# A recurrent recommender on one core: zeros multiplied ahead of the first input, the item part of the attention in another PSUM ring, and the first inputs issued by ScalarE

## The chip, the cores and the metric

The kernel runs on one core of one Trainium2 chip. The metric is the device time of one execution in microseconds (us). The time before is the median of three runs, and one further execution was recorded by the hardware profiler.

## What is computed

For 1024 users with 100 steps of history each, 128 features wide, the reference runs a GRU over the history, scores every state against the candidate item with a small three-layer network, takes a softmax over the steps, pools the states with it, runs a second recurrent layer (AUGRU) whose update gate is weighted by the pooled vector, and puts the result through a three-layer head. Cut to what bears on the first microseconds:

```python
def gru_step(h, x_t):
    gi = x_t @ gru_Wih.T + gru_bih
    gh = h @ gru_Whh.T + gru_bhh
    i_r, i_z, i_n = jnp.split(gi, 3, axis=-1)
    h_r, h_z, h_n = jnp.split(gh, 3, axis=-1)
    r = jax.nn.sigmoid(i_r + h_r)
    z = jax.nn.sigmoid(i_z + h_z)
    n = jnp.tanh(i_n + r * h_n)
    h_new = (1.0 - z) * n + z * h
    return (h_new, h_new)
...
feat = jnp.concatenate([keys, q, keys - q, q * keys], axis=-1)
score = _mlp(feat, [(att_W0, att_b0), (att_W1, att_b1), (att_W2, att_b2)], jax.nn.relu)
score = jnp.where(mask[:, :, None] == 1, score, -jnp.inf)
attn = jax.nn.softmax(score, axis=1)[..., 0]
pooled = jnp.einsum('bt,btd->bd', attn, keys)
```

The part of the first attention layer that depends on the item q alone, `q @ (W_q - W_diff).T + b0`, is the same for all steps. The kernel computes it once; it is called the item part.

## The kernel before

Features lie on the 128 partitions and users on the free axis. The 1024 users are two halves of 512 (`HB`), and each step of the GRU phase works first on half 0, then on half 1. Everything is float32.

**The GRU phase** (`gru_phase`, line 186 on) loops over 100 steps. A step and half has three gates. `gate` (line 504 on) takes one buffer of the PSUM pool `ps` (six buffers, tag "g", called the gates' ring) and adds up one or two products in it: the input x with `wih` and the state h with `whh`. Each product is four matmuls, one for each 32 rows of the output (line 508). At step 0 there is no h, so a gate is one product. ScalarE makes the gates' sigmoid and tanh (lines 520, 539, 540), VectorE the rest of the step (lines 537 or 528, 538, 543 to 545). After the two halves of step s come the attention's matmuls for step s-1 (`attend`, line 670), in two buffers of a second PSUM pool `pa` (two buffers, tag "a"). VectorE adds the item part `q0` to their result one step later (`take`, line 704).

**The start.** SyncE issues the loads in the program's order: `wih` (line 188), x of step 0 for half 0 (line 191), the biases `bih` and `bhh` (line 124, called from 192 and 193), x of step 0 for half 1 (line 195), `whh`, then x of steps 1 and 2 (line 477), the item (line 226) and the attention's weights (lines 124 and 234 to 240). VectorE's first instruction adds the biases into `brz` (line 200). ScalarE's first are its table load and a one-column activation (line 204). GpSimd clears tiles (lines 201 to 215).

**The item part** (`item_part`, line 242 on) runs once, after the gates of step 1 and before the first attention matmuls. For each half it takes a buffer of `pa` for the product `pq` (line 245), and ScalarE copies it with a bias into `q0` (line 248).

**What sets the order.** There is no scheduler at work here (`tc.manual_schedule()`): on each engine the instructions stand in the order in which the Python code names them[...]. The tile framework only adds semaphore waits: for data, and for the buffer of a pool to come free. The pool `wp` (two buffers for each tag) holds VectorE's products `kq` (line 583), which the attention's matmuls read.

After step 99 come the last softmax blocks, the pooling, and the AUGRU phase with PSUM banks chosen by hand (`EARLY_BANKS`, `LATE_BANKS`, `FREE_BANK`). The diff touches none of that code.

Of the kernel before, what the change touches and what calls it, by code (L numbers as in the profile page):

```python
# [9 lines left out]
F32 = mybir.dt.float32  # L10
# [9 lines left out]
P = 128  # L20
B = 1024
T = 100
HB = 512
# [4 lines left out]
R = 32  # L28
# [50 lines left out]
def kernel(ctx: ExitStack, tc: tile.TileContext, a: dict, out: bass.AP):  # L79
# [26 lines left out]
    nc = tc.nc  # L106
# [79 lines left out]
    def gru_phase(pools):  # L186
# [1 line left out]
        nc.sync.dma_start(out=wih, in_=a["wih"])  # L188
        xp = pools.enter_context(tc.tile_pool(name="xp", bufs=8))
        x_first = xp.tile([P, HB], F32, name="x")  # L190
        nc.sync.dma_start(out=x_first, in_=a["hist_x"][0][:, :HB])
        bih = load("bih", [P, 3])
        bhh = load("bhh", [P, 3])
        x_second = xp.tile([P, HB], F32, name="x")
        nc.sync.dma_start(out=x_second, in_=a["hist_x"][0][:, HB:])
        whh = load("whh", [P, 3, P])
        pre = pools.enter_context(tc.tile_pool(name="pre", bufs=1))

# [20 lines left out]
        wp = pools.enter_context(tc.tile_pool(name="wp", bufs=2))  # L219
        sp = pools.enter_context(tc.tile_pool(name="sp", bufs=2))  # L220
        kp = pools.enter_context(tc.tile_pool(name="kp", bufs=3 * NH))
        ps = pools.enter_context(tc.tile_pool(name="ps", bufs=6, space=PSUM))
        pa = pools.enter_context(tc.tile_pool(name="pa", bufs=2, space=PSUM))

        def attention_weights():
            nc.sync.dma_start(out=item, in_=a["item"])
            w0 = load("w0", [P, 4, A0])
            for i in range(NH):
                for f, s in F0[i]:
                    nc.vector.tensor_add(wk[i][:, f], w0[:, 0, s], w0[:, 2, s])  # L230
                    nc.vector.tensor_copy(wkq[i][:, f], w0[:, 3, s])
                    nc.vector.tensor_sub(wq[i][:, f], w0[:, 1, s], w0[:, 2, s])
                    for f1, s1 in F1[i]:
                        nc.sync.dma_start(out=w12[i][f, f1], in_=a["w1"][s, s1])
                    nc.sync.dma_start(out=bm[i][f, :], in_=a["b0"][s, :])
                sc = slice(SC[i], SC[i] + 1)
                for f1, s1 in F1[i]:
                    nc.sync.dma_start(out=w12[i][f1, sc], in_=a["w2"][s1, :])
                    nc.sync.dma_start(out=bm[i][f1, :], in_=a["b1"][s1, :])
                nc.sync.dma_start(out=bm[i][sc, :], in_=a["b2"].partition_broadcast(1))  # L240

        def item_part():
            for i in range(NH):
                pq = pa.tile([P, HB], F32, tag="a", name="pq")
                nc.tensor.matmul(
                    pq, lhsT=wq[i], rhs=item[:, ts(i, HB)], start=True, stop=True
                )
                nc.scalar.activation(q0[:, ts(i, HB)], pq, AF.Identity, bias=bm[i])
# [211 lines left out]
        class Half:  # L460
# [13 lines left out]
            def load(self, t, again=False):  # L474
                if t or again:
                    x = xp.tile([P, HB], F32, name="x")
                    nc.sync.dma_start(out=x, in_=a["hist_x"][t][:, self.cols])
                    self.x[t] = x
# [100 lines left out]
            def product(self, t):  # L579

                h = self.h[t]
                kq = wp.tile([P, HB], F32, name="kq")
                nc.vector.tensor_mul(kq, h, item[:, self.cols])  # L583
                self.first = h, kq

# [238 lines left out]
        for s in range(T):  # L824
# [36 lines left out]
            if s == 0:  # L861
                attention_weights()
            else:
                if not staged:
                    next(rest, None)
                if s == 1:
                    item_part()
                attend(s - 1)
# [403 lines left out]
    with ExitStack() as pools, tc.manual_schedule():  # L1272
        gru_phase(pools)
# [79 lines left out]
```

## Time and profile before

| | us |
|---|---|
| median of three runs | 2031.93 |
| the three runs | 2027.62, 2031.93, 2031.96 |
| the profiled execution, whole | 2054.49 |
| its span, first to last instruction | 2052.7 |
| PE busy from 0 to 10 us | 6.03 |
| PE busy from 10 to 20 us | 10.00 |
| PE busy from 20 to 30 us | 8.36 |
| PE busy from 30 to 40 us | 10.00 |

PE is TensorE's matmuls, PEld its weight loads, DVE is VectorE, ACT ScalarE, POOL GpSimd, SPq and ACTq are the queues of SyncE and ScalarE in which DMAs are issued. Times in the profile count from the first instruction of the span. A timeline row gives the start, the length from the first start to the last end in the row, the engine, the source line, the operation with the tile it writes and those it reads, the shape, the count, and in brackets how long the engine had been idle and what ended that. A matmul in float32 shows as two records for one instruction, so that eight records are one product of a gate with one operand.

### The profile page before, as it was taken

To read this page: it belongs to the slowest core of one execution; us is meant where nothing else is said; L and a number is where in the kernel's file an instruction comes from. 1 tells how busy PE (TensorE), PEld (TensorE's weight loads), DVE (VectorE), ACT (ScalarE), POOL (GpSimd) and SP (SyncE) were. 2 spreads that over 40 slices of the span, in tenths; PEclk is the share of its full clock that TensorE was granted. 3 is DMA by queue.
4 is the path that set the end of the run, shared out by engine and by line. 5 is a ranking of instruction groups with operands and counts; after the bars stand their busy time and mean duration, and the time that the engine had idled before them with its cause. 6 is when DMAs were issued, how large, how long until landed. Compare 5 with 4: busy or idle time off the path is not lost.

```text
span 2052.7 us, 41040 instructions
## 1 busy us (share of the span) xinstructions
PE 1998.8 (97%) x15452; PEld 1049.1 (51%) x15452; DVE 1763.7 (86%) x3066; ACT 824.5 (40%) x1508; POOL 1313.0 (64%) x1291
## 2 busy tenths in 40 slices
PE   8999999999999999999999999998699999999998
PEld 4655433333455544444443333334344556679997
DVE  6888999998999999989999899997377777888886
ACT  3334343333434343434343343343244444445554
POOL 0234939569797969695979787998543354443431
PEclk9999999999999999999999999999799999999999
DMA  4453233332334334333433232333432333333332
GB/s 121 97 115 105 89 105 113 96 93 78 104 113 114 108 109 124 113 99 110 135 105 100 85 99 77 102 105 103 117 101 88 94 110 98 94 102 85 93 72 37
DMA packets 241643, 205.65 MB, mean 100 GB/s; under 512 B 59270, under 2 KB 204394, under 8 KB 241434
## 3 DMA queue, kind: packets, MB, share of 16 engines
q1 hardware_dynamic: 227498, 170.43, 29.4%
q0 software_dynamic: 12352, 32.31, 5.7%
q8 instruction: 123, 2.02, 0.4%
q14 instruction: 86, 0.70, 0.1%
q10 hardware_dynamic: 1584, 0.20, 0.1%
HBM read 146.82 MB, written 54.40 MB: 98 GB/s over the span
## 4 chain that ended last, share of the span: by engine, by line
PE 83%; DVE 9%; issue 2%; DMA 2%; ACT 1%; POOL 1%; another core or an unknown queue 1%; SPq 0%; DVEq 0%; ACTq 0%; POOLq 0%
PE ps L508 42%; PE pm L670 14%; PE ph L1076 5%; PE pr L1076 4%; PE pu L1076 4%; PE pr L1072 4%; PE pu L1072 4%; PE ph L1072 4%; DVE kq L583 1%; DMA rows<-keys_d,idx_k 1%; DVE ps L538 1%; DVE d L544 1%; DVE d L543 1%; DVE u L528 1%; ACT ps L539 1%
## 5 line engine op out<-in xcount | busy, mean ns | idle before, releaser
L508 PE MATMUL ps<-x,wih 128*32 128x512 f32 x4800 | 778.3, 595 | 4.6 <-DMA x<-in_hist_x 4.0
L508 PE MATMUL ps<-hn,whh 128*32 128x512 f32 x4752 | 768.1, 592 | 0.0
L508 PEld LDWEIGHTS ps<-x,wih 128*32 128x32 f32 x4800 | 260.2, 110 | 291.0 <-issue 270.2
L508 PEld LDWEIGHTS ps<-hn,whh 128*32 128x32 f32 x4752 | 258.2, 110 | 280.1 <-issue 271.9
L539 ACT ACTIVATE ps<-ps,bih 128x512 f32<-128x512 f32 x200 | 132.4, 662 | 546.5 <-DVE ps L538 546.5
L493 POOL TENSOR_TENSOR xm<-x,m 128x512 f32<-128x512 f32 x200 | 248.1, 1240 | 121.7 <-DMA m<-mask_d 60.8
L494 POOL TENSOR_TENSOR hist<-hist,xm 128x512 f32<-128x512 f32 x200 | 269.7, 1349 | 15.7
L174 POOL DMA_INDIRECT rows<-keys_d,idx_k x220 | 213.9, 972 | 86.5 <-POOL rows L173 50.0
L607 POOL TENSOR_TENSOR pooled<-pooled,kw 128x512 f32<-128x512 f32 x191 | 257.6, 1349 | 15.0
L670 PE MATMUL pm<-hn,wk 128*32 128x512 f32 x1200 | 257.1, 592 | 4.0 <-DVE f L704 2.3
L606 POOL TENSOR_TENSOR kw<-kt,e 128x512 f32<-128x512 f32 x191 | 220.1, 1153 | 62.2 <-DVE e L779 62.1
L670 PE MATMUL pm<-kq,wkq 128*32 128x512 f32 x1200 | 257.2, 592 | 0.0
L520 ACT ACTIVATE r<-ps,brz 128x512 f32<-128x512 f32 x200 | 137.6, 688 | 285.6 <-PE ps L508 285.1
L670 PE MATMUL pm<-mv,w 128*32 128x512 f32 (+1 forms) x808 | 240.5, 592 | 8.2 <-DVE e L760 8.2
L583 DVE TENSOR_TENSOR kq<-hn,item 128x512 f32<-128x512 f32 x200 | 233.0, 1204 | 0.0
L1084 ACT ACTIVATE c<-ph,bh 128x96 f32<-128x96 f32 (+41 forms) x198 | 96.4, 487 | 292.6 <-PE ph L1076 248.3
L173 POOL COPY rows<-rest 128x1 f32<-128x1 f32 x188 | 35.3, 188 | 215.4 <-DVE rest L1113 211.7
L543 DVE TENSOR_TENSOR d<-hn,ps 128x512 f32<-128x512 f32 x198 | 136.1, 687 | 34.9 <-ACT ps L539 32.4
L1100 DVE TENSOR_TENSOR pu<-pu,c 128x96 f32<-128x96 f32 (+41 forms) x197 | 88.2, 448 | 86.0 <-ACT c L1084 77.4
L538 DVE TENSOR_TENSOR ps<-ps,u 128x512 f32<-128x512 f32 x200 | 140.0, 700 | 23.7 <-PE ps L508 3.1
L544 DVE TENSOR_TENSOR d<-ps,d 128x512 f32<-128x512 f32 x200 | 138.3, 691 | 22.7 <-ACT ps L540 3.4
L704 DVE TENSOR_TENSOR f<-pm,q 128x512 f32<-128x512 f32 x200 | 128.0, 681 | 26.5 <-PE pm L670 26.4
(180 smaller groups left out, 3101.5 us busy)
## 6 DMA issues: line engine op xcount, KB each, us to landing
x<-in_hist_x SPq DMA_DIRECT2D x212, 256.0 KB
keys_d<-kt SPq DMA_DIRECT2D x48, 1024.0 KB
m<-mask_d SPq DMA_DIRECT2D x200, 128.0 KB
rows<-keys_d,idx_k POOLq DMA_INDIRECT x220
s_b<-mv SPq DMA_DIRECT2D x200, 8.0 KB
keys_d<-kt SPq DMA_DIRECT2D x32, 64.0 KB
at<-att_d SPq DMA_DIRECT2D x34, 48.0 KB
mask_i<-in_mask SPq DMA_DIRECT2D x8, 200.0 KB
```

Source lines behind the costliest of these rows:

```text
L174: nc.gpsimd.indirect_dma_start(out=r[:, at, :], out_offset=None, in_=keys_d[q], in_offset=bass.IndirectOffsetOnAxis(ap=idx_k[:, k, i : i + ...
L493: nc.gpsimd.tensor_mul(d, x, m)
L494: nc.gpsimd.tensor_add(acc, acc, d)
L508: nc.tensor.matmul(p[ts(q, R), :], lhsT=w[:, g, ts(q, R)], rhs=v, start=(j == 0), stop=(j == len(parts) - 1),)
L538: nc.vector.tensor_add(pi, pi, u)
L544: nc.vector.tensor_mul(d, pz, d)
L583: nc.vector.tensor_mul(kq, h, item[:, self.cols])
L606: eng.tensor_mul(d, k, w)
L607: eng.tensor_add(acc, acc, d)
L670: nc.tensor.matmul(p[i][s, :], lhsT=w[:, s], rhs=v, start=start, stop=stop)
L1072: nc.tensor.matmul(p, lhsT=m[:, 1, :], rhs=k, start=True, stop=False)
L1076: nc.tensor.matmul(p, lhsT=m[:, 0, :], rhs=v, start=False, stop=True)
```

## The change

Three things are edited, and a fourth follows from the first.

1. After the pools are opened, VectorE clears a 128x512 tile `idle`, and PE multiplies it by itself: eight matmuls of the gates' shape into two buffers of `pa`. Nobody reads the result.
2. The two loads of x for step 0 are issued by ScalarE's queue in place of SyncE's. They stand where they stood in the code, which is ahead of ScalarE's table load.
3. The product `pq` of the item part takes its two buffers from the gates' ring `ps` in place of `pa`.
4. `idle` lives in the buffers of `kq`, which for that get an explicit tag of the same name.

```diff
         x_first = xp.tile([P, HB], F32, name="x")
-        nc.sync.dma_start(out=x_first, in_=a["hist_x"][0][:, :HB])
+        nc.scalar.dma_start(out=x_first, in_=a["hist_x"][0][:, :HB])
         bih = load("bih", [P, 3])
         bhh = load("bhh", [P, 3])
         x_second = xp.tile([P, HB], F32, name="x")
-        nc.sync.dma_start(out=x_second, in_=a["hist_x"][0][:, HB:])
+        nc.scalar.dma_start(out=x_second, in_=a["hist_x"][0][:, HB:])
         whh = load("whh", [P, 3, P])
...
         pa = pools.enter_context(tc.tile_pool(name="pa", bufs=2, space=PSUM))
+
+        idle = wp.tile([P, HB], F32, tag="kq", name="idle")
+        nc.vector.memset(idle, 0.0)
+        for _ in range(2):
+            p = pa.tile([P, HB], F32, tag="a", name="pd")
+            for q in range(P // R):
+                nc.tensor.matmul(
+                    p[ts(q, R), :], lhsT=idle[:, ts(q, R)], rhs=idle, start=True, stop=True
+                )
...
             for i in range(NH):
-                pq = pa.tile([P, HB], F32, tag="a", name="pq")
+                pq = ps.tile([P, HB], F32, tag="g", name="pq")
                 nc.tensor.matmul(
                     pq, lhsT=wq[i], rhs=item[:, ts(i, HB)], start=True, stop=True
                 )
...
-                kq = wp.tile([P, HB], F32, name="kq")
+                kq = wp.tile([P, HB], F32, tag="kq", name="kq")
```

In the changed kernel the new lines are 225 to 232, and what followed is nine lines further down: the gates' matmuls are at line 517, the item part at 254 and 257, the attention at 679.

## The prediction

> **What bounds the kernel now.** I read the page first: engine shares, then the chain that ended last.
>
> ```profile
> span 2052.7 us, 41040 instructions
> PE 1998.8 (97%) x15452; PEld 1049.1 (51%) x15452; DVE 1763.7 (86%) x3066; ACT 824.5 (40%) x1508; POOL 1313.0 (64%) x1291
> ...
> PE 83%; DVE 9%; issue 2%; DMA 2%; ACT 1%; POOL 1%; another core or an unknown queue 1%; SPq 0%; DVEq 0%; ACTq 0%; POOLq 0%
> ```
>
> TensorE (PE) is busy for 97% of the span and is 83% of the chain. So whatever is added to or taken from PE's own stream moves the end; DVE at 86% has room. The change touches only the first 30 us, so I next asked who PE waits for in the first 60 us. The answer has two rows (columns: total us, times, longest):
>
> ```profile
> PE ps L508 <- DMA x<-in_hist_x: 4.0, 1, 4.0
> PE pm L670 <- ACT q L248: 1.6, 1, 1.6
> ```
>
> These are the two waits that the change is about. Between them, and after 25.85 us, PE stands still for nothing: the table by stretches has PE busy 12.85 of 12.85 us from 9.35 to 22.20, and 14.15 of 14.15 from 25.85 to 40.
>
> The timeline of the weight loads shows the pace of the first gates (columns: start, us). One row is four 32-column weights, and a gate's product with one operand is two such groups:
>
> ```profile
> 8.21 0.23 PEld L508 LDWEIGHTS ps<-x,wih 128*32 128x32 f32 x4 [0.63 <-issue]
> 9.06 0.23 PEld L508 LDWEIGHTS ps<-x,wih 128*32 128x32 f32 x4 [0.63 <-issue]
> 9.66 0.14 PEld L508 LDWEIGHTS ps<-x,wih 128*32 128x32 f32 x4 [0.37 <-issue]
> 10.09 0.14 PEld L508 LDWEIGHTS ps<-x,wih 128*32 128x32 f32 x4 [0.29 <-issue]
> ```
>
> A group takes 0.855 us up to 9.06 and 0.43 us from 9.66. The step of 0.60 between them is part slow, part fast: 0.345 us slow, so PE changes pace at 9.40, which is 5.43 us after its first matmul at 3.97. That costs 5.43/2 = 2.7 us.
>
> Then the rows that decide when the zeros can start, SyncE's issues and VectorE's first instruction:
>
> ```profile
> 0.75 0.39 SPq L188 DMA_DIRECT2D wih<-in_wih  x1
> 1.19 0.42 SPq L191 DMA_DIRECT2D x<-in_hist_x  x1
> 1.66 0.42 SPq L124 DMA_DIRECT2D bih<-in_bih  x1
> 2.12 0.43 SPq L124 DMA_DIRECT2D bhh<-in_bhh  x1
> ...
> 5.27 0.16 DVE L200 TENSOR_TENSOR brz<-bih,bhh 128x2 f32<-128x2 f32 x1 [5.27 <-DMA bhh<-in_bhh]
> ```
>
> VectorE does nothing until 5.27 us: its first instruction waits for bhh, which comes 5.27 - 2.12 = 3.15 us after its issue. x comes earlier, at 3.83 on the chain.
>
> Last, the item part:
>
> ```profile
> 22.23 1.98 PE L245 MATMUL pq<-item,wq 128*128 128x512 f32 x4
> 25.11 1.27 ACT L248 ACTIVATE q<-pq,bm 128x512 f32<-128x512 f32 x2
> 25.85 0.62 PE L670 MATMUL pm<-hn,wk 128*32 128x512 f32 x2 [1.64 <-ACT q L248]
> ```
>
> pq holds both buffers of pool pa, so the first attention matmul stands 1.64 us until ScalarE has read pq.
>
> [...]
>
> **The change, part by part.** Write S for the start of PE's first matmul, W for the slow time after it. A stream of G groups ends at S + 0.4285 G + W/2 (0.4285 us is a fast group: 10.09, 10.52, 10.95 in the weight loads).
>
> *Zeros.* `nc.vector.memset(idle)` stands at line 226 of the changed kernel, after the addition into brz (line 200), on the same engine. VectorE can't clear the tile before bhh has come. So the zeros don't fill the wait for x; they begin after it. bhh's issue moves up one slot (x has left SyncE's queue), to 1.66. With the same 3.15 us it comes at 4.81. Then brz 0.16, memset 0.48 (the row of TENSOR_SCALAR 128x512 at line 537[...]), 0.03 to the next engine as from ACT L539 to DVE L543: PE starts at 5.48, 1.51 us later than 3.97. Eight instructions are two gate products, 4 groups, so 4 x 0.4285 = 1.71 us on top. All slow they take 3.42 us and end at 8.90; the remaining slow time then falls on the gates. **At the first gates: +1.51 + 1.71 = +3.22 us.** Nothing hides it, as x is there from about 4 us. Bounds: bhh might come as early as x's own delay allows (1.66 + 2.64 = 4.30; start 4.9) or no earlier than now (5.27; memset 0.6; start 6.1), -0.6 to +0.6. [...] That zeros don't count as work for the clock is a rival below.
>
> *Item part in the ring ps.* pq takes two of the gates' six buffers. The built order gives the new waits. The first attention matmul no longer waits for q: **-1.64 us**. What is late next: pq's first tile waits for r of step 1 (ended 21.41), its second for d (ended 21.74), both before 22.23. In step 2 a gate of the first half waits for q's first half (about 25.8); PE reaches it no sooner than 24.2 + 3.43 (attention) + 3 x 0.857 = 30.2. The second half's waits for q at 26.4, also long past. The adders (f, line 704) stand behind the attention matmuls, which end after 27. So nothing takes the stall's place, and by step 3 both kernels wait for the same instructions; the banks at the phase change are the same too.
>
> *First inputs on ScalarE's queue.* ScalarE issues two DMAs ahead of its table load: about 0.5 us each (line 1229: 1.53 us for three), table load 1.28, activation 0.2: done at 3.3 us, while r is needed after the first gate, never before 5.9. Hidden; without that cover about 1.0 us. x issued at about 0.75 instead of 1.19 gains nothing, as PE then waits for zeros. On SyncE's queue, bih and bhh move up by one slot (counted above), whh and all later loads by two (0.95 us); each was needed later than it came.
>
> *The kq tag* lets idle share kq's two buffers: free at line 583, 16.78 us.
>
> **Sum.** +1.51 + 1.71 - 1.64 = +1.58 us against the profiled execution: 2052.7 becomes 2054.3, and 2054.49 of that run's whole time becomes 2056.1. The profiled time lies 22.6 us above the median; the change's rows lie in the first 30 us and don't scale with that, so I add the same to the median: 2031.93 + 1.58 = **2033.5 us**, 0.08%.
>
> **Rivals.**
> *A, it does what it says*: the zeros start with the other engines at 0.75. Memset ends at 1.26, slow zeros at 4.68; -2.71 + 1.71 - 1.64 = -2.64: 2029.3. For it speaks only the description; against it the order on VectorE. 0.04.
> *B, part of the gain is missing*: another wait at the first attention matmul (the attention's weights, issued until 18.91, or kq), or zeros that don't bring the clock up, so that the gates start slow at 8.90: 4.93 - 1.64 = +3.3. Either gives about 2035.2. Against: the loads have 5 us[...]. 0.17.
> *C, slower*: bhh is late. [...] Each us of delay at line 200 is one us at the end. Measurably slower (6.1 us) needs PE's start at 3.97 + 6.1 + 1.64 - 1.71 = 10.0, bhh at 9.3, 7.7 us after issue instead of 3.15. The first 0.7 MB at 300 to 400 GB/s (the DMA lines of the first 6 us) take about 2 us. At 9.3 the time is 2038. 0.05.
> *Forecast*: 0.74.
>
> **How the numbers follow.** About 0.3% is what a measurement of this kernel can tell from no change: 6.1 us. The forecast and B lie within it, A too. C and noise make 0.06 slower, noise 0.03 faster, 0.91 same. The range: forecast with its bounds, -1.6 to +1.3 about 2033.5, gives 2031.9 to 2034.8; the three runs shown spread 4.3 us, mostly downward; up it reaches B and some of C. 2029.0 to 2037.0.
>
> **What the profile will show.** The first matmul is of idle, near 5.5 us, behind VectorE's memset; the first gate near 8.9; brz near 4.8. [...] The attention matmul after pq has no wait for q; PE's first 26 us end some 1.6 us later than now. I am wrong if the zeros start before 4.3 us, if another wait of over 0.5 us stands between pq and attention, or if anything after step 3 differs by more than the runs do.

## The result, and the profile after

| | before, us | after, us |
|---|---|---|
| median (22 runs each, taken together on one chip) | 2031.70 | 2034.95 |
| range of the runs | 2027.62 to 2034.29 | 2032.80 to 2037.72 |
| the profiled execution, whole | 2054.49 | 2033.47 |
| its span | 2052.7 | 2031.7 |

The ratio of the runs is 1.0019, with a 95% interval of 1.0013 to 1.0024: the changed kernel is slower by 2.6 to 4.9 us; the medians lie 3.3 us apart. The forecast was 1.58 us slower. The two spans must not be compared: in the profiled execution of before PE stood 12.3 us at the change of phase (`PE pr L1076 <- DVE h L1022`), which is far behind the edited code; in that of after the same wait took 0.7 us. The experiments below form three sets, each on a chip of its own with the kernel before beside it; on the second chip every kernel took some 28 us more, the one before too, so medians are compared only within a set.

First the page of after: the share of PE and its part of the chain are as they were.

```profile
span 2031.7 us, 41074 instructions
PE 1994.4 (98%) x15468; PEld 1017.2 (50%) x15468; DVE 1762.0 (87%) x3067; ACT 824.8 (41%) x1508; POOL 1315.8 (65%) x1291
...
PE 81%; DVE 11%; issue 3%; DMA 2%; ACT 1%; POOL 1%; SPq 0%; DVEq 0%; ACTq 0%; POOLq 0%
```

PE's waits in the first 60 us of after (total us, times, longest) answer to the two rows of before:

```profile
PE pd L230 <- DVE idle L226: 5.8, 1, 5.8
PE pq L254 <- issue: 0.3, 1, 0.3
```

The wait for x (4.0 us) has become a wait for the zeros (5.8 us), and the wait for q (1.6 us) is gone, with a new, shorter one at `pq`. The timeline of after (start, length) shows why the zeros are late:

```profile
0.74 0.42 ACTq L191 DMA_DIRECT2D x<-in_hist_x  x1
...
1.66 0.42 SPq L124 DMA_DIRECT2D bhh<-in_bhh  x1
...
5.01 0.16 DVE L200 TENSOR_TENSOR brz<-bih,bhh 128x2 f32<-128x2 f32 x1 [5.01 <-DMA bhh<-in_bhh]
5.23 0.48 DVE L226 MEMSET idle<- 128x512 f32 x1
...
5.77 1.08 PE L230 MATMUL pd<-idle 128*32 128x512 f32 x4 [5.77 <-DVE idle L226]
```

VectorE stands at line 200 until bhh is there, clears the tile behind that, and PE starts at 5.77 (before: 3.97). The weight loads of the first gates give the pace again:

```profile
9.18 0.20 PEld L517 LDWEIGHTS ps<-x,wih 128*32 128x32 f32 x4 [0.66 <-issue]
10.03 0.20 PEld L517 LDWEIGHTS ps<-x,wih 128*32 128x32 f32 x4 [0.66 <-issue]
10.77 0.12 PEld L517 LDWEIGHTS ps<-x,wih 128*32 128x32 f32 x4 [0.54 <-issue]
11.20 0.12 PEld L517 LDWEIGHTS ps<-x,wih 128*32 128x32 f32 x4 [0.31 <-issue]
```

The eight instructions on zeros take 3.41 us (5.77 to 9.18), all at half pace (0.85 us a group), and the step from 0.85 to 0.43 us for a group lies between 10.03 and 10.77. The trace's record of the granted clock (the share of TensorE's full pace that it was given, 1.00 or 0.50 here) puts it at 10.63, 4.86 us after PE's first matmul (before: 5.43). Then the stretch around the item part, from the same timeline:

```profile
25.27 0.69 ACT L529 ACTIVATE r<-ps,brz 128x512 f32<-128x512 f32 x1
...
26.05 1.96 PE L254 MATMUL pq<-item,wq 128*128 128x512 f32 x4 [0.31 <-issue]
...
27.94 0.62 PE L679 MATMUL pm<-hn,wk 128*32 128x512 f32 x2
...
29.67 1.27 ACT L257 ACTIVATE q<-pq,bm 128x512 f32<-128x512 f32 x2
```

The attention starts 1.9 us after `pq` and doesn't wait for q, which is copied at 29.67. But `pq` itself starts only when r of step 1, half 1, has been read out (25.27 + 0.69 = 25.96), a wait that before did not have. The profile names no releaser for it ("issue"). That it is this r, whose buffer `pq` takes over, is read from the times: in eight profiles `pq` starts 0.10 us after this r ends, and nowhere sooner in a kernel that has it in the gates' ring.

One row of each step, the start of r (ACT line 529, before 520) for half 0, tells where the time stays. Times of before: step 8 at 114.21, step 26 at 365.76, step 30 at 423.12, step 99 at 1378.71.

| r of half 0 in step | 0 | 2 | 8 | 26 | 30 | 99 |
|---|---|---|---|---|---|---|
| after less before, us | +5.06 | +1.55 | +1.55 | +1.62 | +3.44 | +2.57 |

From step 2 to step 27 the difference is the forecast's 1.58 within 0.04 us. Between steps 27 and 28 another 1.8 us come, where both kernels run the same instructions. The table by stretches shows these 1.8 us (after the stretch: busy time and count for PE, PEld, DVE, ACT, POOL, then the granted clock PEclk, the DMA share, GB/s). Of after:

```profile
389.50:392.50 3.00, 0.93 (x12) 0.21 (x9) 2.91 (x5) 0.38 (x1) 2.84 (x4) 1.00 0.00 0
393.00:396.20 3.20, 3.20 (x20) 0.95 (x16) 2.88 (x5) 1.24 (x2) 0.74 (x1) 0.50 0.01 3
396.40:399.00 2.60, 2.60 (x32) 0.96 (x28) 1.62 (x3) 0.00 (x0) 0.00 (x0) 1.00 0.00 0
```

and of before:

```profile
388.00:390.40 2.40, 0.33 (x8) 0.13 (x8) 2.33 (x5) 0.14 (x1) 2.32 (x3) 1.00 0.00 0
390.40:394.00 3.60, 3.60 (x36) 1.31 (x39) 3.18 (x6) 1.24 (x2) 1.49 (x2) 1.00 0.02 5
```

In both, PE stands for about 2 us while VectorE transposes the scores of a softmax block. In after the clock is then granted at one half for a stretch, 20 matmul records in 3.2 us; in before it stays at 1.00, 36 records in 3.6 us. The row that ends the stall in after:

```profile
392.05 0.59 PE L679 MATMUL pm<-mv,w 128*32 128x512 f32 x1 [2.07 <-DVE e L769]
```

The clock's record has the half-rate stretch from 392.93 to 396.34: 3.41 us at half pace, in which half of them, 1.7 us, are lost. Behind step 30 the difference drifts by about a microsecond, as it does between two executions of one kernel: the second profile of before, below, stands at -0.43 us in step 30 and at -1.54 in step 99.

### The profile page after: what moved, and what is told of

It is laid out like the page before. It is cut to its first block, busy times and chain, and to the rows that moved or that the text cites. A ratio compares the mean times of both kernels' runs of the same rounds, so it can differ in the third digit from the quotient of the medians.

```text
span 2031.7 us, 41074 instructions
## 1 busy us (share of the span) xinstructions
PE 1994.4 (98%) x15468; PEld 1017.2 (50%) x15468; DVE 1762.0 (87%) x3067; ACT 824.8 (41%) x1508; POOL 1315.8 (65%) x1291
## 4 chain that ended last, share of the span: by engine, by line
PE 81%; DVE 11%; issue 3%; DMA 2%; ACT 1%; POOL 1%; SPq 0%; DVEq 0%; ACTq 0%; POOLq 0%
PE ps L517 39%; PE pm L679 14%; PE ph L1085 5%; PE pr L1085 5%; PE pu L1085 4%; PE ph L1081 4%; PE pu L1081 4%; PE pr L1081 4%; DVE kq L592 2%; DVE ps L547 1%; DMA rows<-keys_d,idx_k 1%; DVE d L553 1%; DVE d L552 1%; DVE u L537 1%; ACT ps L548 1%
## 5 line engine op out<-in xcount | busy, mean ns | idle before, releaser
L517 PE MATMUL ps<-x,wih 128*32 128x512 f32 x4800 | 757.2, 593 | 0.7 <-DVE u L537 0.7
L517 PE MATMUL ps<-hn,whh 128*32 128x512 f32 x4752 | 748.8, 592 | 0.0
L517 PEld LDWEIGHTS ps<-x,wih 128*32 128x32 f32 x4800 | 240.7, 110 | 298.6 <-issue 262.3
L517 PEld LDWEIGHTS ps<-hn,whh 128*32 128x32 f32 x4752 | 239.1, 110 | 292.0 <-issue 278.5
L537 DVE SCALAR_TENSOR_TENSOR u<-ps,bhh,r 128x512 f32<-128x512 f32 x198 | 146.7, 741 | 5.5 <-PE ps L517 5.3
```

The source lines that it names most:

```text
L517: nc.tensor.matmul(p[ts(q, R), :], lhsT=w[:, g, ts(q, R)], rhs=v, start=(j == 0), stop=(j == len(parts) - 1),)
L537: nc.vector.scalar_tensor_tensor(out=u, in0=ph, scalar=bhh[:, 2:3], in1=r, op0=ALU.add, op1=ALU.mult,)
```

## The experiments

The first set takes the change apart (before has a median of 2030.82 us there). "Step 8" is always the start of r in step 8 less that of the profile of before.

**The item's part alone.**

```diff
-                pq = pa.tile([P, HB], F32, tag="a", name="pq")
+                pq = ps.tile([P, HB], F32, tag="g", name="pq")
```

> Only the item part is moved to the gates' ring; no zeros, x on SyncE's queue. Theory (PE's stream sets the end, the 1.64 us wait for q is gone for good): the first attention matmul comes at 24.2 us instead of 25.85, the step times from step 4 on are 1.6 us earlier than in the profile of before, time 2030.1. Rival (another wait takes its place at step 2): the steps stand where they stood, time 2031.7. If the surplus of the whole change over the forecast (3.25 us measured, 1.58 forecast) comes from the ring, this kernel is slower than before by 0 to 1.7 us.

Measured: median 2027.78, ratio 0.9987 (0.9981 to 0.9994); step 8 at -2.58. PE's only wait in its first 60 us:

```profile
PE ps L508 <- DMA x<-in_hist_x: 4.0, 1, 4.0
```

and the first attention matmul in its timeline:

```profile
23.80 0.62 PE L670 MATMUL pm<-hn,wk 128*32 128x512 f32 x2
```

Nothing takes the place of the wait for q. PE started 0.07 us later than before, and the clock came 0.83 us sooner, worth 0.42; the rest, -2.58 - 0.07 + 0.42 = -2.23, or **-2.2 us**, is the item's part, and not 1.64. The weight loads of before show the missing piece, a second wait that lies behind the first (the timeline of its weight loads):

```profile
25.85 0.14 PEld L670 LDWEIGHTS pm<-hn,wk 128*32 128x32 f32 x4 [2.47 <-ACT q L248]
...
26.43 0.11 PEld L670 LDWEIGHTS pm<-hist,w 128*32 128x32 f32 x1 [0.36 <-ACT q L248]
```

The attention of half 1 needs the other buffer of `pa` and waits for q's second half. From the first attention matmul to r of step 2 before takes 31.87 - 25.85 = 6.02 us, this kernel 29.29 - 23.80 = 5.49: another 0.53 us. A count of PE's idle time misses it, as the prediction's 14.15 busy of 14.15 us did, since matmuls of the first half still ran.

**The zeros alone** (with the kq tag, all else as before).

```diff
+        idle = wp.tile([P, HB], F32, tag="kq", name="idle")
+        nc.vector.memset(idle, 0.0)
+        for _ in range(2):
+            p = pa.tile([P, HB], F32, tag="a", name="pd")
...
```

> Only the zeros are added; the item part stays in pa, x on SyncE's queue. Theory: bhh comes at 5.27 as before, zeros start at 6.0, first gate at 9.5. The sum over PE's stream alone gives +3.8 us. With the chain of VectorE and ScalarE, which starts a whole 5.3 us late because all zeros run at half pace, the wait for q is not 1.64 but about 2.6, and the first attention matmul comes at 30.6, +4.8 us; time 2036.5. Rival (zeros cost PE nothing, since it would have waited anyway): +0 to +0.5, time 2032.

Measured: median 2039.46, ratio 1.0036 (1.0023 to 1.0050); step 8 at +6.30. PE's waits up to 60 us,

```profile
PE pd L230 <- DVE idle L226: 6.2, 1, 6.2
PE pm L679 <- ACT q L257: 2.7, 1, 2.7
```

and three stretches of its table (columns as above):

```profile
27.00:31.00 4.00, 1.25 (x7) 0.22 (x6) 3.64 (x7) 2.36 (x4) 0.00 (x0) 1.00 0.34 57
31.00:34.40 3.40, 3.40 (x20) 1.35 (x18) 0.55 (x1) 0.06 (x1) 0.00 (x0) 0.50 0.67 158
34.50:38.00 3.50, 3.50 (x40) 1.62 (x36) 1.53 (x3) 0.00 (x0) 0.00 (x0) 1.00 0.43 153
```

The wait for q grew from 1.6 to 2.7 us, as expected (2.6): ScalarE's and VectorE's part of steps 0 and 1 begins five microseconds late (r of step 0 at 11.16, before 5.96) while PE comes only some three late. A half-rate stretch follows this stall too (granted clock 0.50 from 31.0 to 34.4), and a second one the stall at 394 us (0.77 on average from 393 to 399); the expected 2036.5 had neither. Without the item's edit the zeros cost 6 us at step 8.

**The change without the zeros.** The rest of the changed kernel stays.

```diff
-        idle = wp.tile([P, HB], F32, tag="kq", name="idle")
-        nc.vector.memset(idle, 0.0)
-        for _ in range(2):
...
```

> The change without the zeros: item part in the gates' ring, x issued by ScalarE. Theory: the zeros alone make the change slower, so this is faster than before by the 1.64 us of the item part and by at most 0.4 us of the earlier x; time 2029.7 to 2030.1, ratio to before 0.9991. Rival (x on a second queue[...] delays the first gate): the first gate comes later than 3.97 us and the ratio is above 0.9992.

Measured: median 2028.59, ratio 0.9990 (0.9981 to 0.9998); step 8 at -2.53. It differs from the item's part alone only by the queue of the first inputs. x is issued at 0.74 instead of 1.19, and PE's first matmul, which waits for it, still starts at 4.17 instead of 4.04 us:

```profile
4.17 1.08 PE L508 MATMUL ps<-x,wih 128*32 128x512 f32 x4 [4.17 <-DMA x<-in_hist_x]
```

With x on SyncE's queue this start lies between 3.97 and 4.44 us in five profiles, so the 0.13 us mean nothing. The queue gains nothing, and costs nothing that can be measured.

**The zeros cleared first.** The tile gets a place of its own, and its memset stands ahead of the addition that waits for bhh.

```diff
+        idle = pre.tile([P, HB], F32, name="idle")
+        nc.vector.memset(idle, 0.0)
         nc.vector.tensor_add(brz, bih[:, 0:2], bhh[:, 0:2])
...
-        idle = wp.tile([P, HB], F32, tag="kq", name="idle")
-        nc.vector.memset(idle, 0.0)
```

> The change with its memset ahead of the addition into brz on VectorE, in a tile of its own; all else the same. Theory (the order on VectorE is what made the change slower): zeros start at about 1.3 us and end at 4.7, the first gate starts there[...]. PE's stream alone gives -2.6 us against before; the chain of VectorE and ScalarE, whose head moves by +0.7, leaves about -2.0; time 2029.1 to 2029.7. Rival (zeros don't count for the clock, so the gates still start at half pace): [...]the kernel stands at -0.9 (4.68 - 3.97 - 1.64): 2030.8.

Measured: median 2029.69, ratio 0.9995 (0.9989 to 1.0002); step 8 at -2.59. Its timeline:

```profile
0.93 0.48 DVE L201 MEMSET idle<- 128x512 f32 x1 [0.93 <-PEq L1349]
...
1.47 3.64 PE L230 MATMUL pd<-idle 128*32 128x512 f32 x16 [1.47 <-DVE idle L201]
...
4.88 2.35 PE L517 MATMUL ps<-x,wih 128*32 128x512 f32 x12
```

So the zeros do what the change says once VectorE clears them first: they fill the wait for x, and the clock comes at 6.65, 5.18 us after the zeros but only 1.77 us after the first gate, where the item's part alone took 4.60 from its first gate (4.04 to 8.64): **zeros bring the clock up**. Yet step 8 is no earlier than with the item's edit alone: the first gate starts 0.84 us later than there (4.88 against 4.04), and 0.5 us are lost to the chain of the other engines (below). And the median is 1.9 us above that kernel's. In the profile the stall at 385.7 is followed by a half-rate stretch, and the mean granted clock of the 21 runs each, 0.99471 against 0.99552, makes 0.00081 x 2030 = 1.6 us of it the clock's:

```profile
385.50:388.00 2.50, 0.42 (x7) 0.19 (x8) 2.43 (x5) 0.14 (x1) 2.42 (x3) 1.00 0.00 0
389.00:392.30 3.30, 3.30 (x20) 1.08 (x16) 2.80 (x5) 1.24 (x2) 0.41 (x1) 0.50 0.01 2
```

The second set (before 2059.18 us) was made to find what decides the half-rate stretch near 390 us: a delay of the clock that is the same in every execution, which would tie the stretch to the kernel's own lengths (Theory L), or chance (Theory C).

**Half of the zeros**, in the changed kernel.

```diff
-        for _ in range(2):
+        for _ in range(1):
             p = pa.tile([P, HB], F32, tag="a", name="pd")
```

> The change with one tile of zeros, four matmuls, in place of two. Both theories: the stream ahead of the gates is two groups shorter, so the step times from step 4 on are about 0.86 us earlier than with the whole change (fast groups; the slow time stays the same), perhaps 0.5 more as the chain of VectorE and ScalarE starts 1.71 us earlier. Theory L[...]: 2.4 to 3.0 us faster than the whole change, about 2032, mean granted clock over the runs above 0.9952. Theory C[...]: 0.9 to 1.4 faster, the half-rate window as frequent as with the whole change, mean clock 0.9948.

Measured: median 2060.84, ratio 1.0008 (1.0001 to 1.0014); step 8 at +0.09, and a half-rate stretch from 391.5 us on, after which +1.86. PE's start at 5.97, two groups fewer, and the clock 3.24 us after the first matmul, against 4.86 in after. A delay that is the same in every execution (Theory L) is thereby refuted. The median lies 2.4 us below that of the changed kernel on this chip, which was Theory L's number; but the half-rate stretch, whose absence was to bring it, is there, and the scatter of the runs (-0.5 to 4.8 us, 95%, by resampling them) tells no more.

**Half of the zeros, cleared first**: the same edit in the kernel with the early memset.

> The change with the memset ahead of brz on VectorE, in a tile of its own, and four zero matmuls in place of eight. Zeros start at 1.47, end at 3.2, ahead of x (about 4.1): the first gate is as early as without zeros. If the short pause doesn't hold back the clock, the pace changes near 6.6 us (5.1 after the first zeros) in place of 8.6; the chain of VectorE and ScalarE then starts at about 6.1 and not at 6.9, and the first attention matmul comes near 23.0 us: 0.8 us ahead of the kernel with the item part alone (23.80), 2.85 ahead of before; time 0.8 below the item part alone, near 2027.5. Rival (the pause starts the count anew): the pace changes no sooner than 8.6 and nothing is gained over the kernel without zeros, 23.8 us and about 2028.5. [...]

Measured: median 2058.48, ratio 1.0001 (0.9993 to 1.0009); step 8 at -2.98, no half-rate stretch in the GRU phase. The zeros end at 3.4 and PE waits 0.67 us for x; the clock comes 6.27 us after the first matmul, at 7.74, between the expected 6.6 and the rival's 8.6. The expected median, 0.8 us below the item's part alone, did not come: the kernel can't be told from before.

**The changed kernel and the kernel before, again.** No edit.

> The changed kernel itself, for a second profile and for its times beside the other three on one chip. Theory L: the pace changes again 4.3 to 5.4 us after the first zeros, the 2.07 us stall near 390 [...]is followed by 3.41 us at half rate; mean clock 0.9948, ratio to before 1.0015 to 1.0022. [...]

Measured: median 2063.22, ratio 1.0016 (1.0007 to 1.0025); step 8 at +1.89, step 30 at +3.68; again a half-rate stretch, at 393.6.

> The kernel before itself, for a second profile without the 12.3 us wait of the first one at the phase change. Both theories: ratio 1.0000 within 0.0007; first attention matmul between 25.4 and 26.4 us; PE waits twice for the item part, on q's first half (1.64 us) and then, behind its second attention matmul, on q's second half (0.3 to 0.5 us). Theory L: [...]no half-rate window after it, mean clock 0.9952. [...]

Measured: median 2059.75, ratio 1.0004 (0.9996 to 1.0012); step 8 at +0.03; no half-rate stretch in the GRU phase.

The third set (before 2030.44 us) takes the stall itself away. In steps 27 and 35 PE gets one more matmul of the gates' shape, which writes into a quarter of a bank that is begun afresh later in the step. Its operand is the state that VectorE finishes in the middle of the stall at step 27. (At step 35 the state is there earlier: in both profiles the extra matmul runs at once, and PE then still stands 1.85 and 0.87 us.)

```diff
                     for q in range(2, P // R):
                         more((QA, QB)[j].index(q), q)
+                        if turn == 0 and q == 2 and t in (26, 34):
+                            h = halves[0].h[t + 1]
+                            pack(0, QB[0], wk[0], h, True, True)
```

> The changed kernel, with one extra matmul in each of the two longest stalls of TensorE in the GRU phase (steps 27 and 35, 2.07 and 1.6 us of waiting for the softmax's first products): it multiplies the hidden state that VectorE has just finished into a quarter of a bank that is overwritten later in the same step, so that the stall is cut in two and its end doesn't move. Theory W: the part of the loss that comes after step 3 is the stretch of 3.4 us at half clock which follows such a stall, 1.7 us. Then no half-rate stretch stands behind the stall at 390 us, the GRU's steps stay at +1.6 us against the kernel before up to its end, and the median is 1.2 to 2 us below that of the changed kernel in this call. Theory D: the later loss lies elsewhere (transfers, the change of phase), and the half-rate stretch of the profile was that one execution's. Then the median is within 0.5 us of the changed kernel's.

> The kernel before with the item's part in the gates' ring alone, and the same two extra matmuls. Theory W: it has little to lose there: its profile showed a half-rate stretch after the stall at 498 us, its times as a whole showed no loss, so 0 to 0.8 us below the same kernel without them; and the changed kernel with the matmuls stays 4.0 to 4.5 us above this one, which is the distance at step 3 of their profiles (1.6 and -2.6 us against the kernel before). Theory D: no difference from the same kernel without them, and the changed kernel with them stays 5.5 to 6.5 us above this one.

> The changed kernel as it is, to compare the two with the extra matmuls on the same chip: 3 to 4 us over the kernel before on a chip like the first, and a half-rate stretch behind the stall near 390 us if Theory W holds of most executions.

> The item's part in the gates' ring alone, again: 2 to 3 us below the kernel before, first packed matmul of the attention 2.1 us sooner, and no half-rate stretch near 390 us if the placing of these stretches is a property of the kernel; either way, if it is chance.

Measured, with step 8 and step 30 of the profiled executions:

| kernel | median, us | ratio (95%) | step 8 | step 30 |
|---|---|---|---|---|
| after | 2035.42 | 1.0024 (1.0017 to 1.0030) | +1.33 | +3.09 |
| after, stalls filled | 2032.15 | 1.0009 (1.0000 to 1.0017) | +0.83 | +0.96 |
| item's part alone | 2027.96 | 0.9988 (0.9981 to 0.9995) | -2.96 | -2.92 |
| item's part alone, stalls filled | 2028.67 | 0.9990 (0.9984 to 0.9997) | -1.88 | -1.83 |

The filled stall of after in its timeline:

```profile
389.47 0.69 DVE L554 TENSOR_TENSOR hn<-ps,d 128x512 f32<-128x512 f32 x1
390.08 0.71 DVE L768 STREAM_TRANSPOSE pt<-s_b 128x512 f32<-128x512 f32 x1
...
390.21 1.05 PE L679 MATMUL pm<-hn,wk 128*32 128x512 f32 x2 [1.02 <-DVE hn L554]
...
391.26 0.59 PE L679 MATMUL pm<-mv,w 128*32 128x512 f32 x1
```

the stretch behind it,

```profile
391.50:394.90 3.40, 3.40 (x36) 1.25 (x32) 2.98 (x6) 1.24 (x2) 1.32 (x2) 1.00 0.02 5
```

and the stall and the stretch behind it of the unfilled kernel on this chip:

```profile
389.50:392.50 3.00, 0.93 (x11) 0.34 (x12) 2.83 (x6) 0.03 (x1) 2.84 (x4) 0.99 0.00 0
392.60:395.90 3.30, 3.30 (x20) 1.08 (x16) 2.98 (x5) 1.24 (x2) 0.95 (x1) 0.51 0.03 7
```

PE's longest idle time there goes from 2.07 us to 1.02, the end of the stall doesn't move, the clock stays at 1.00, and the median falls by 3.3 us. Theory D (the later loss lies elsewhere) falls. Theory W (the later loss is the stretch at half clock behind the stall) holds, with several numbers off. The fall was to be 1.2 to 2.0 us; the two filled kernels were to lie 4.0 to 4.5 us apart and lie 3.5; the filled kernel's steps were to stay at +1.6 and stand at +0.83 to +0.96, as its clock came after 3.16 us; and after was to stand 3 to 4 us over the kernel before and stands 5.0 over it. The mean granted clock that was noted for every run says how much of the fall is the clock's: 0.99480 over 20 runs of after, 0.99577 over 13 of the filled one, a difference of 0.00097 x 2030 = 2.0 us. For the remaining 1.3 us between the two medians no profile shows a place; resampling the runs puts the fall between 1.8 and 4.3 us (95%), so they may be scatter. In the kernel with the item's part alone the matmuls changed little (+0.7 us, the intervals overlap): it had little to lose there.

## Why the prediction was right, and where it was not

The changed kernel came out 3.25 us slower, for a forecast of 1.58. By the profiles 1.55 us of this stand at step 8, as forecast, and 1.8 come between steps 27 and 28, where the forecast had nothing. The forecast's own bounds ended at 2034.8 (the share of the half pace in them was shown by no trace); 2034.95 lies just above them, and inside 2029.0 to 2037.0 because that range left room for noise and rivals.

**The zeros start late: right.** VectorE stands behind bhh, as forecast. bhh came 3.35 us after its issue (5.01 - 1.66) rather than 3.15, and from there to PE 0.76 us passed rather than 0.67; the memset itself took the 0.48 us that were priced. The start is 5.77 instead of 5.48: +1.80 for the forecast +1.51.

**The zeros cost four groups: right**, and they bring the clock up (1.77 us after the first gate where they ran ahead of it). Where they run all at half pace, the half pace is paid once, as the forecast had it. The formula S + 0.4285 G + W/2, made for one kernel, can now be tested on eleven profiles. Take for each the change of PE's start against 3.97, the zeros at 0.4285 us a group (plus PE's wait for x where they ended too soon), the change of half the time worked at half pace against 5.43/2, and -2.2 for the item's part:

| kernel | start | zeros | half pace | item | sum | step 8 measured | rest |
|---|---|---|---|---|---|---|---|
| after | +1.80 | +1.71 | -0.28 | -2.2 | +1.03 | +1.55 | 0.52 |
| after, second | +1.97 | +1.71 | -0.05 | -2.2 | +1.43 | +1.89 | 0.46 |
| after, third | +1.83 | +1.71 | -0.53 | -2.2 | +0.81 | +1.33 | 0.52 |
| after, stalls filled | +1.92 | +1.71 | -1.13 | -2.2 | +0.30 | +0.83 | 0.53 |
| half of the zeros | +2.00 | +0.86 | -1.10 | -2.2 | -0.44 | +0.09 | 0.53 |
| zeros first | -2.50 | +1.71 | -0.13 | -2.2 | -3.12 | -2.59 | 0.53 |
| zeros first, half | -2.50 | +0.86 + 0.67 | +0.08 | -2.2 | -3.09 | -2.98 | 0.11 |
| no zeros | +0.20 | | -0.49 | -2.2 | -2.49 | -2.53 | -0.04 |
| item alone | +0.07 | | -0.42 | -2.2 | -2.55 | -2.58 | -0.03 |
| item alone, second | +0.14 | | -0.95 | -2.2 | -3.01 | -2.96 | 0.05 |
| item alone, filled | +0.47 | | -0.10 | -2.2 | -1.83 | -1.88 | -0.05 |

The item's 2.2 comes from the first run of the item's part alone; in the other three without zeros the rest is 0.05 us or less. The zeros alone, which keep the wait for q, fit as well: +2.19 + 1.71 - 0.53, 1.1 for the longer wait and 1.7 for the half-rate stretch at 31 us make +6.2, and step 8 is at +6.3.

**"Nothing takes the stall's place": wrong by half a microsecond.** The item's edit was worth 2.2 us instead of 1.64, since the second wait for q was overlooked. In six of the seven profiles with zeros and the item's edit together 0.46 to 0.53 us come back. In after they are two new waits, the 0.31 us at `pq` and this one in step 1 (its timeline):

```profile
15.49 0.60 PE L517 MATMUL ps<-x,wih 128*32 128x512 f32 x4
...
16.09 0.16 PEld L517 LDWEIGHTS ps<-hn,whh 128*32 128x32 f32 x8 [0.91 <-DVE hn L554]
```

The two groups start 0.60 us apart, 0.17 more than the 0.43 of a fast group; 0.31 + 0.17 = 0.48. The wait at `pq` is in the other five as well, and a step of 0.59 to 0.60 us in four of them. The prediction had seen that `pq` would wait for r of step 1, and took the times of before (21.41 against 22.23) to show a slack of 0.8 us. But it had moved PE alone. In before some 3.4 us of the half pace (5.96 to 9.40) fall on gates after the first r; in after that time is spent on zeros. So the first r comes 5.06 us later than in before,

```profile
11.02 0.69 ACT L529 ACTIVATE r<-ps,brz 128x512 f32<-128x512 f32 x1 [7.85 <-PE ps L517]
```

```profile
5.96 0.69 ACT L520 ACTIVATE r<-ps,brz 128x512 f32<-128x512 f32 x1 [3.72 <-PE ps L508]
```

while PE's own stream is only 1.80 + 1.71 - 0.28 = 3.2 us later; the chain of ScalarE and VectorE through the first two steps becomes the one that ends last. The two errors are of opposite sign and nearly equal, and with the later start (+0.29) and the earlier clock (-0.28) they give +1.55 at step 2 for the forecast 1.58. The sum was right partly by luck, because its terms failed in pairs; and the three profiles of the changed kernel stand at +1.33, +1.55 and +1.89, so that 0.03 us is the agreement of one execution. W, for which the forecast took the 5.43 us of before, ran from 3.16 to 6.27 us.

**"By step 3 both kernels wait for the same instructions": right as to the instructions, wrong as to the time.** They do wait for the same ones, for as long (2.07 us at 390), but what follows the wait differs: one stretch at half clock, 1.7 us. By the prediction's own clause (anything after step 3 that differs by more than the runs do) this is where it was wrong. That the stretch is caused by the stall is shown by the filled stall (granted clock 1.00 from 391.5 to 394.9, and 0.51 from 392.6 to 395.9 in the unfilled kernel). That it is there in most executions of the changed kernel is what three profiles out of three say, and in the third set the mean clock of all runs (0.99480 over 20 of after, 0.99551 over 61 of before: 1.4 us); on the second chip the mean clock doesn't separate the kernels (0.99076 over 17 runs of after, 0.99040 over 53 of before).

What decides whether it comes was not shown. The length of the stall alone doesn't: 2.07 us near 390 are followed by half rate in after and not in before, and before then has 2.31 us near 1391 and stays at 1.00 up to 1419. The clock's records of after and before show where the pace changed: in after at 112, 113, 406, 407, 419, 421 and 590 times 3.413 us behind the first change (10.63), in before likewise at whole multiples, from 413 to 597, behind 9.40. So the stall's place is counted from that change. The distance from it to the stall at 390 us, in the eleven profiles that have the whole stall before any other half-rate stretch:

| kernel | distance, us | half rate behind it |
|---|---|---|
| item alone, twice | 377.03, 377.67 | no, no |
| no zeros | 377.16 | no |
| zeros first, half | 377.72 | no |
| before, twice | 378.37, 378.83 | no, no |
| after, three times | 378.94, 379.34, 379.46 | yes, yes, yes |
| zeros first | 379.08 | yes |
| half of the zeros | 379.19 | yes |

The answer changes between 378.83 and 378.94 us. Why there, no run shows: none set the place on purpose. Nor does it carry over to other lengths: in after 1.93 us near 1347 were not followed by half rate, and in the item's part alone 1.98 us near 498 were. In the kernel after with its stalls filled the stall would have begun at 380.15 by this count, beyond the change, and with the extra matmul in it (PE's longest idle time 1.02 us) it has no half-rate stretch behind it; with the item alone, filled, it is 376.74, and none either. The ends of matmuls are modelled in the profile, so its hundredths decide nothing here.

The distance is about a constant of the kernel less half the slow time W (after 381.6 to 381.8, item alone 379.3 to 379.4, before 381.1 to 381.5), and W ran from 3.16 to 6.27 us in these runs. So the kernel sets the range in which the distance can fall, and each execution picks the value in it. How often each kernel is hit was not measured beyond the mean clock.

**The rivals.** A (it does what it says) is the kernel with the early memset, and even that stands no earlier at step 8 than the item's edit alone. B's zeros that don't bring the clock up are refuted (1.77 us after the first gate); its place near 2035 was reached, but by a cause it didn't name. C did not happen: line 200 ran at 5.01. For the queue: issued 0.45 us sooner in the kernel without zeros, x came no sooner (4.17 us, against 4.04 in the item's part alone).

**The best version** measured is the item's edit alone, at 0.9987 and 0.9988 of the kernel before on two chips, 3.0 and 2.5 us by the medians. By the mean granted clock of the runs (0.99552 against 0.99518, and 0.99558 against 0.99551) 0.7 and 0.1 us of these are the clock's, which leaves about 2.3 us both times. No form with zeros was faster than before by more than its interval. Half of the zeros, cleared first, has the earliest step 8 (-2.98, against -2.96 and -2.58 for the item's edit alone), and with the half pace of before it would stand some 0.9 us ahead of the item's edit (-2.98 - 0.08 against -2.58 + 0.42). Its median, 1.0001 of before on the second chip, doesn't bear this out; the two were not run on one chip, so that stays open.

## What to carry to other kernels

Filler that is to cover a wait must not stand behind that same wait, or a later one, on the engine that prepares it: look at what is ahead of its first instruction in that queue (here a sum that waited for bhh until 5.01 us held the memset to 5.23). When a start is delayed, move the other engines' chains as well as the bottleneck's, and look at a second buffer's wait behind the first before pricing a stall by the idle time that the profile shows. In this kernel a stall of 2.07 us on PE cost 1.7 us more than its length in five profiles of eleven (3.41 us at half rate behind it); one matmul in its middle took that away.

## What the runs showed of the hardware

- From TensorE's first matmul to full pace it took 3.16 to 6.27 us in fourteen profiles (the longest with 0.67 us of waiting in it); where zeros ran ahead of the first gate, the half pace ended 1.77 us after that gate.
- Later, in the GRU phase, a stall of 2.07 us near 390 us was followed by 3.41 us at half rate in five profiles of eleven (in after from 392.93 to 396.34), and one of 1.98 us by another (item alone, at 498 us, granted clock 0.50 from 500.2 to 503.5); in after, one of 2.66 us near 1393 was followed by 3.41 us from 1396.44 on. In after 1.63 and 1.93 us, and in before 1.72, 1.94, 2.07 and 2.31 us, were followed by none.
- A load of 128 rows of 12 bytes (bhh) was used 3.15 us after its issue in before and 3.35 in after. x of 256 KB, issued 0.45 us sooner on another queue, was used no sooner (4.07 and 4.17 us in two profiles, against 3.97 to 4.44 in five).
- The scores' transfer ahead of the softmax's transposition at step 35 ended PE's wait after 1.63, 1.62 and 2.65 us in the three profiles of after: about a microsecond that comes and goes with the execution.
